# Inverse square roots by logarithm and exponential of one ScalarE table set, in a two-layer spectral MetaFormer

## The chip, the cores and the metric

One core of one Trainium2 chip runs the whole network in one launch. The metric is the device time of the program in microseconds; the median of three runs of the kernel before is 5417.38 us (5405.69 to 5420.78). The engines are named as in the profile: PE is TensorE's matmuls and PEld its weight loads, DVE is VectorE, ACT is ScalarE, POOL is GpSimd, SP is SyncE, which issues the DMAs.

## The reference

The input is eight images of 128 x 128 pixels with 96 channels. Two layers of the same form follow each other; for each:

```python
x = x + conv(_ln_c(x))                  # layer norm over the 96 channels, eps 1e-6
t = t + ffn(_ln_t(t))                   # layer norm over the 96 channels, eps 1e-5

# conv
x_pre = scale * relu(x @ w1.T)**2 + bias                   # 96 -> 192 channels
xf = rfft2(x_pre)
gctx = mean(x); sctx = mean(relu(bn(x @ sp_w.T)))           # over the pixels; bn uses rsqrt(bn_var + 1e-5)
r = softmax(fc2(soa(fc1([gctx, sctx]))), over 3 scales)     # one gate per image
comb = sum over the scales of r * filter
y = irfft2(xf * comb) @ w2.T

# ffn, every product in a quantised 8-bit float, sums in a quantised 16-bit one
y = fc2(relu(fc1(q(x)) + b1)) + b2
```

A layer norm is `(v - mean) / sqrt(var + eps)`. It needs one inverse square root per pixel, and there are 2 layers x 8 images x 16,384 pixels x 2 norms of them. The batch norm of the gate's context needs one inverse square root per channel and layer.

## The kernel before

The work is cut into 16 jobs (2 layers x 8 images), and each job into 16 groups of 8 image rows (`NRG = 16`). Four stages are written as generators whose `yield`s cut them into numbered steps:

- `pixels` (P): loads 8 rows, takes their statistics (L369), normalises on GpSimd (`xn_a`, L441), transposes (L445, read out on ScalarE, L448), multiplies by w1 (L456), takes ReLU (`r`, L459) and the square (`xs`, L463) on ScalarE, adds and subtracts rows (`sd`, L476/L477), and does the Fourier transform along one axis (L486, read out by ScalarE's `lo`, L500, and VectorE's `at`, L502/L503).
- `gate` (G): only at the last group of an image. Matmuls (L521 to L540), a softmax with an exponential on ScalarE (L551), sums on GpSimd (L554/L555), a reciprocal (L557) and the weights `rw` (L560 to L565) on VectorE.
- `frequencies` (F): the second axis of the transform (L627), the filters (L594, L614, read out by `cf`, L634), their complex products on VectorE (`pr`, L645 to L649) and GpSimd (`xf`, L657), the second projection (L698/L703, read out by `zt`, L713) and the inverse transform (L717). The last of the 16 chunks of an image has five columns in place of four.
- `tokens` (S): the last inverse transform (L746), the residual (L755) and its statistics, normalisation into 8-bit floats half on VectorE (L770) and half on ScalarE (L764), transposes (L778/L781), the feed-forward network (L788 to L814; `y` L791 and `h` L798 on ScalarE, `a` L794 on VectorE), and the output (L819).

A fifth list, `Norms.steps` (N), does the inverse square roots of a tick for P and S together, on tiles of 128 x 16 (or 128 x 8, when only one of the two is active). It has three steps. N 0 makes the variance on VectorE (L391 to L395). N 1 takes its square root on ScalarE (L397). N 2 takes the reciprocal on VectorE (L399), improves it with one Newton step (L401, L402, L407) and makes the shift for S (L405, L406).

The order of the work is written out by hand. One tick advances every stage by one group, and the lists `TICK`, `RAMP` and `TAIL` say which step of which stage is recorded in which place; `tc.manual_schedule()` keeps that order, so each engine runs its instructions in the order of the list. Stages lag behind each other by whole ticks (the third number of an entry), and `BANKS` gives each matmul output one of four PSUM bank pairs. In `TICK`, N 1 stands between the transposes' read-out (P 4) and ReLU (P 6):

```python
("P", 4, 1), ("G", 3, -1), ("N", 1, 0), ("P", 0, 3), ("P", 6, 0),
("P", 16, -1), ("N", 2, 0), ("S", 9, 0), ("G", 4, -1), ("P", 17, -1), ("P", 18, -1),
```

ScalarE evaluates Sqrt and Exp from tables, and the two lie in different table sets. So ACT_TABLE_LOAD instructions stand in the program wherever the function changes: one before the softmax's exponential of a gate (L551) and one before the next square root (L397), 16 of each, and one for the first square root of all, which is the batch norm's in the set-up (`prepare`, L268, with its reciprocal on L269).

Of the kernel before, what the change touches and what calls it, by code (L numbers as in the profile page):

```python
# [13 lines left out]
AF = mybir.ActivationFunctionType  # L14
# [160 lines left out]
def metaformer_kernel(ctx: ExitStack, tc: tile.TileContext, x, cst, layers, out):  # L175
    nc = tc.nc
# [8 lines left out]
    def bank2(name):  # L185
        return pp.tile([128, 2, 512], F32, name=name, tag=f"d{banks[name]}")

    ident = const.tile([128, 128], F32, name="ident")
    make_identity(nc, ident)
    ident8 = const.tile([128, 128], F8, name="ident8")  # L190
# [52 lines left out]
    def prepare(us, l, p):  # L243

        wt = {}

        def load(name, shape, view, pool=us):
            t = pool.tile(shape, F32, name=f"{name}_{l}" if pool is const else name)
            nc.sync.dma_start(t, view)
            return t  # L250

        def kept(name, shape, dtype=F32):
            wt[name] = const.tile(shape, dtype, name=f"{name}_{l}")
            return wt[name]

        def row(v, n):
            return v.partition_broadcast(n)


        K1 = C + 1  # L260
        gam = load("gam", [K1, SC], row(p["conv_bn_gamma"], K1))
        bet = load("bet", [K1, SC], row(p["conv_bn_beta"], K1))
        bmu = load("bmu", [K1, SC], row(p["conv_bn_mean"], K1))
        bva = load("bva", [K1, SC], row(p["conv_bn_var"], K1))
        bns = us.tile([K1, SC], F32, name="bns")
        t0 = us.tile([K1, SC], F32, name="bn_t0")
        nc.vector.tensor_scalar(bva, bva, 1e-5, None, ALU.add)
        nc.scalar.activation(t0, bva, AF.Sqrt)  # L268
        nc.vector.reciprocal(bns, t0)  # L269
        nc.vector.tensor_tensor(t0, bns, bns, ALU.mult)  # L270
        nc.vector.tensor_tensor(t0, t0, bva, ALU.mult)
        nc.vector.tensor_scalar(t0, t0, -0.5, 1.5, ALU.mult, ALU.add)
        nc.vector.tensor_tensor(bns, bns, t0, ALU.mult)
        nc.vector.tensor_tensor(bns, bns, gam, ALU.mult)
        nc.vector.tensor_tensor(t0, bmu, bns, ALU.mult)

        raw = us.tile([C, WE], F32, name="raw")
        nc.sync.dma_start(raw[:, :M], p["conv_w1"])
        spw = load("spw", [C, SC], p["conv_sp_w"])
        nc.vector.tensor_tensor(raw[:, M:], spw, bns[:C], ALU.mult)  # L280
        fc1g = load("fc1g", [C, RHID], p["conv_fc1"][:C, :])
        fc1s = load("fc1s", [SC, RHID], p["conv_fc1"][C:, :])

        cen = us.tile([C, C], F32, name="cen")
        nc.vector.tensor_scalar(cen, ident[:C, :C], -1.0 / C, None, ALU.add)
        ps = bank2("ps_w")
        mm(ps[:C, 0, :WE], cen, raw, start=True, stop=True)
        mm(ps[:C, 1, :RHID], cen, fc1g, start=True, stop=True)
        w1 = kept("w1", [K1, WE])
        nc.scalar.copy(w1[:C], ps[:C, 0, :WE])  # L290
        nc.vector.memset(w1[C:], 0.0)
        nc.vector.tensor_tensor(w1[C:, M:], bet[C:], t0[C:], ALU.subtract)
        nc.scalar.mul(kept("fc1g", [C, RHID]), ps[:C, 1, :RHID], 1.0 / (H * W))
        nc.scalar.mul(kept("fc1s", [SC, RHID]), fc1s, 1.0 / (H * W))
        nc.sync.dma_start(kept("fc2", [RHID, NS * M]), p["conv_fc2"])
        nc.sync.dma_start(kept("mlp_s", [RHID, 1]), row(p["conv_mlp_scale"], RHID))
        nc.sync.dma_start(kept("mlp_b", [RHID, 1]), row(p["conv_mlp_bias"], RHID))

        soa_s = load("soa_s", [128, 1], row(p["conv_soa1_scale"], 128))
        nc.vector.tensor_scalar(kept("dft", [128, 128]), kt["dft"], soa_s, None, ALU.mult)  # L300
        dc = kept("dc", [HH, 1])
        nc.sync.dma_start(dc, row(p["conv_soa1_bias"], HH))
        nc.vector.tensor_scalar(dc, dc, 2.0, None, ALU.mult)


        nc.sync.dma_start(kept("w2a", [128, C]), p["conv_w2"][:128, :])
        nc.sync.dma_start(kept("w2c", [128, C]), p["conv_w2"][64:, :])
        w2b = kept("w2b", [128, 2 * C])
        nc.vector.memset(w2b, 0.0)
        nc.sync.dma_start(w2b[:64, :C], p["conv_w2"][128:, :])  # L310
        nc.sync.dma_start(w2b[64:, C:], p["conv_w2"][:64, :])

        def quantised(name, shape, view):
            t = us.tile(shape, F32, name=f"{name}_f")
            nc.sync.dma_start(t, view)
            q = kept(f"{name}_q", shape, F8)
            nc.vector.tensor_copy(q, t, saturate=False)
            return q

        quantised("f1", [C, HID], p["ffn_W1"])  # L320
        quantised("f2", [128, HID // 128, C], p["ffn_W2"].rearrange("(k p) c -> p k c", p=128))
        b1q = quantised("b1", [128, HID // 128], p["ffn_b1"].rearrange("(k p) -> p k", p=128))
        b2q = quantised("b2", [128, C], p["ffn_b2"].partition_broadcast(128))
        nc.vector.tensor_copy(kept("b1", [128, HID // 128]), b1q)
        nc.vector.tensor_copy(kept("b2", [128, C], F16), b2q)
        return wt

    with tc.tile_pool(name="us", bufs=2) as us:
        pad = us.tile([NKW, GP - 2 * NHS, M], F32, name="pad", bufs=1)
        nc.gpsimd.memset(pad, 0.0)  # L330
        wts, cws = [], []
        for l, p in enumerate(layers):
            wts.append(prepare(us, l, p))
            cws.append(load_filters(us, l, p))
        constants("fwd", "inv", "idft", "rh", "mask")
        for l in range(len(layers)):
            small_filters(us, l, cws[l], pad)
# [21 lines left out]
    class Norms:  # L359
# [13 lines left out]
        def steps(self):  # L373

            if not self.slots:
                yield from [None] * 3
                return
            sl = slice(min(self.slots), max(self.slots) + 1)

            def new(name):  # L380
                return ab.tile([128, 2, RG], F32, name=f"n_{name}")

            add, mult = ALU.add, ALU.mult
            tt, stt = nc.vector.tensor_tensor, nc.vector.scalar_tensor_tensor
            me, mo = self.st[:, sl, :, 1], self.st[:, sl, :, 4]
            d, v, a, rs, nb = (new(i) for i in ("d", "v", "a", "rs", "nb"))
            sm = ab.tile([128, 2, RG, 2], F32, name="n_sm")
            self.sm, self.a, self.rs, self.nb = sm, a, rs, nb
            d, v, a, rs, sm = (i[:, sl] for i in (d, v, a, rs, sm))

            tt(sm, self.st[:, sl, :, 1:3], self.st[:, sl, :, 4:6], add)  # L391
            tt(d, me, mo, ALU.subtract)
            stt(v, d, 0.25, d, mult, mult)
            stt(v, sm[:, :, :, 1], 1.0 / C, v, mult, add)
            tt(v, v, eps[:, sl], add)  # L395
            yield
            nc.scalar.activation(a, v, AF.Sqrt)  # L397
            yield
            nc.vector.reciprocal(rs, a)  # L399

            stt(a, rs, -0.5, rs, mult, mult)  # L401
            tt(a, a, v, mult)  # L402
            if 1 in self.slots:
                nb = self.nb[:, 1]
                stt(nb, self.sm[:, 1, :, 0], -0.5, self.rs[:, 1], mult, mult)  # L405
                stt(nb, self.a[:, 1], 1.5, nb, add, mult)  # L406
            stt(rs, a, 1.5, rs, add, mult)  # L407
            yield
# [489 lines left out]
```

## Time and profile before

| what | before |
|---|---|
| median of three runs | 5417.38 us |
| span of the profiled execution | 5425.3 us |
| ACT_TABLE_LOAD | 33 of 1283 ns |
| Sqrt on L397 | 297, mean 219 ns |
| reciprocal on L399 | 297, mean 237 ns |
| exponential of the softmax, L551 | 16 of 684 ns |

The profile is of one execution. Its page gives the busy time of each engine, the span in 40 slices, the chain of waits that ended last, and the costliest groups of instructions. A group's row ends with the idle time of its engine just ahead of it and the instruction that ended it. An instruction in order of time that had to wait has that wait in square brackets, with what ended it. In a table of stretches each row has the stretch, its length, the busy time of TensorE, its weight loads, VectorE, ScalarE and GpSimd (with the instructions in brackets), the granted TensorE clock as a share of the full one, the share of the DMA engines, and GB/s. Line numbers are those of the kernel before.

### The profile page before, as it was taken

Reading aid. Unit: us, or ns where it says so; the run is one execution under the profiler, and the core shown is the slowest. Engines: PE = TensorE matmul, PEld = TensorE weight load, DVE = VectorE, ACT = ScalarE, POOL = GpSimd, SP = SyncE. Lnnn points to the kernel's source line nnn. Section 1 sums busy time; section 2 is a strip of 40 time slices with the busy share of each in tenths; the row PEclk is TensorE's granted clock in tenths of the full one; section 3 lists DMA queues with packets and bytes.
Section 4 is the critical chain, followed back from the end, with each engine's and each line's share of the span. In section 5 each row is a group of like instructions: output and inputs, shape, how many; then the busy total and the mean of one; then the engine's idle time right before and its main releaser. Section 6 shows DMA issues by size and latency. Waiting matters only on the chain.

```text
span 5425.3 us, 116490 instructions
## 1 busy us (share of the span) xinstructions
PE 5111.2 (94%) x41192; PEld 4031.7 (74%) x41192; DVE 4532.2 (84%) x14113; ACT 4400.2 (81%) x6882; POOL 2663.7 (49%) x1911
## 2 busy tenths in 40 slices
PE   4899999999999999999999999999999999998976
PEld 2577777878787787878778787877878787787743
DVE  3887888888888888888888888888888888888876
ACT  2654688888888888878888888888888888887778
POOL 0354555555555555545555555555555555554421
PEclk9999999999999999999999999999999999999987
DMA  5566777777676676767777776777777677766643
GB/s 143 163 163 156 182 197 193 205 190 210 184 209 196 192 206 182 212 179 202 205 199 201 189 212 183 208 197 196 201 191 212 177 209 199 197 195 174 179 122 108
DMA packets 908042, 1020.15 MB, mean 188 GB/s; under 512 B 67106, under 2 KB 839954, under 8 KB 907122
## 3 DMA queue, kind: packets, MB, share of 16 engines
q1 hardware_dynamic: 907460, 1012.71, 67.6%
q8 instruction: 327, 5.36, 0.4%
q14 instruction: 255, 2.09, 0.1%
HBM read 598.62 MB, written 413.84 MB: 187 GB/s over the span
## 4 chain that ended last, share of the span: by engine, by line
PE 73%; DVE 9%; issue 6%; ACT 5%; POOL 3%; DMA 2%; SPq 1%; POOLq 0%; DVEq 0%; ACTq 0%
PE pw L456 13%; PE py L627 12%; PE pf L614 7%; PE pz L703 6%; PE pi L717 6%; PE pz L698 6%; PE pa L486 5%; PE ps_r L746 5%; PE pm L788 5%; PE po L805 4%; PE pt_a L445 3%; PE pt_c L778 2%; DVE pr L645 1%; POOL ut L594 1%; DMA u_d<-u 1%
## 5 line engine op out<-in xcount | busy, mean ns | idle before, releaser
L657 POOL TENSOR_TENSOR xf<-pr 128x768 f32<-128x768 f32 (+2 forms) x544 | 957.9, 1764 | 320.6 <-DVE pr L649 280.7
L456 PE MATMUL pw<-w,xT 97*128 97x240 f32 x4096 | 935.2, 372 | 22.2 <-ACT y L791 14.0
L819 POOL TENSOR_TENSOR y<-xr,o 128x768 f32<-128x768 f32 x256 | 460.0, 1797 | 967.3 <-DVE o L816 930.4
L441 POOL TENSOR_TENSOR xn_a<-xt,n_rs 128x768 f32<-128x768 f32 x256 | 414.0, 1617 | 1016.8 <-DVE n_rs L407 832.5
L645 DVE TENSOR_TENSOR pr<-py,cf 128x768 f32<-128x768 f32 (+2 forms) x544 | 502.1, 923 | 469.3 <-PE py L627 430.3
L456 PEld LDWEIGHTS pw<-w,xT 97*128 97x128 f32 x4096 | 773.5, 194 | 154.3 <-ACT y L791 18.4
L627 PE MATMUL py<-k_fwd,al 128*128 128x128 f32 x6272 | 838.9, 283 | 1.7 <-ACT zt L713 1.7
L791 ACT CAST y<-pm 128x1024 f16<-128x1024 f32 x768 | 771.6, 1006 | 61.7 <-PE pm L788 60.9
L798 ACT ACTIVATE h<-a 128x1024 fp8e5<-128x1024 f16 x768 | 808.7, 1056 | 4.4 <-DVE a L794 3.7
L627 PEld LDWEIGHTS py<-k_fwd,al 128*128 128x128 f32 x6272 | 751.2, 193 | 43.7 <-issue 7.3
L459 ACT ACTIVATE r<-pw 128x960 f32<-128x960 f32 x512 | 496.4, 970 | 350.0 <-PE pw L456 349.9
L594 POOL TENSOR_TENSOR ut<-ut,rw 112x768 f32<-112x768 f32 (+1 forms) x256 | 490.0, 1914 | 317.3 <-DMA ut<-u_d 171.7
L698 PE MATMUL pz<-w2b,xf 128*128 128x192 f32 (+1 forms) x2112 | 553.8, 344 | 9.2 <-DVE hr L532 5.4
L788 PE MATMUL pm<-xq,f_q 96*128 96x512 fp8e5 x1536 | 474.3, 390 | 84.5 <-DVE pr L649 41.5
L698 PEld LDWEIGHTS pz<-w2b,xf 128*128 128x128 f32 (+1 forms) x2112 | 337.7, 190 | 185.1 <-issue 144.7
L614 PEld LDWEIGHTS pf<-k_rh,ut 48*128 48x128 f32 x6272 | 377.6, 190 | 119.1 <-issue 69.0
L794 DVE TENSOR_SCALAR a<-y,b 128x1024 f16<-128x1024 f16 x768 | 427.2, 556 | 43.9 <-ACT y L791 43.9
L614 PE MATMUL pf<-k_rh,ut 48*128 48x128 f32 x6272 | 433.4, 284 | 31.3 <-POOL ut L594 31.3
L463 ACT ACTIVATE xs<-r 128x768 f32<-128x768 f32 x512 | 428.1, 836 | 0.6
L634 ACT COPY cf<-pf 128x768 f32<-128x768 f32 (+2 forms) x544 | 399.8, 795 | 34.5 <-PE pf L614 34.4
L717 PE MATMUL pi<-zt,k_inv 128*128 128x384 f32 (+1 forms) x1024 | 423.0, 538 | 0.0
L781 ACT ACTIVATE xq<-pt_c 96x1024 fp8e5<-96x1024 f32 x256 | 260.9, 1019 | 181.0 <-PE pt_c L778 181.0
(126 smaller groups left out, 10648.8 us busy)
## 6 DMA issues: line engine op xcount, KB each, us to landing
a_d<-at SPq DMA_DIRECT2D x256, 768.0 KB
al<-a_d SPq DMA_DIRECT2D x960, 192.0 KB
v<-y_d SPq DMA_DIRECT2D x256, 384.0 KB
y_d<-yt SPq DMA_DIRECT2D x480, 192.0 KB
ut<-u_d SPq DMA_DIRECT2D x240, 336.0 KB
xt<-in_x_dram SPq DMA_DIRECT2D x512, 96.0 KB
xr<-in_x_dram SPq DMA_DIRECT2D x128, 384.0 KB
mid<-y SPq DMA_DIRECT2D x128, 384.0 KB
```

What stands on the lines that cost most here:

```text
L456: mm(o, xT[:, 4 * a + 2 * i + j, :], wt["w1"], start=True, stop=True)
L459: nc.scalar.activation(r.rearrange("p a s c -> p a (s c)"), pw, AF.Relu)
L594: nc.gpsimd.tensor_tensor(ut[:, :n], ut[:, :n], _bc_mid(jb.rw, n), ALU.mult)
L614: mm(pf[:nm, i, t * 128 : (t + 1) * 128], utf[64 * i : 64 * i + NHS, cs], kt["rh"][64 * i : 64 * i + NHS, :], start=True, stop=True,)
L627: mm(py[:nm, t, e, :], alf[:, e, cs], kt["fwd"][:, e, :], start=True, stop=True)
L645: nc.vector.tensor_tensor(p0, yq, crb, ALU.mult)
L657: nc.gpsimd.tensor_tensor(xv[:q, te], pr[:q, 0, te].rearrange("p t r k -> p t (r k)"), pr[:q, 1, te].rearrange("p t r k -> p t (r k)"), AL ...
L698: mm(o[:, : u * C], xf[:kb, 1, e, :], wt["w2b"][:kb, : u * C], start=True, stop=False,)
L717: mm(pi[:, e, : n * C], kt["inv"][:, e, :], zt[:, e, : n * C], start=True, stop=True)
L788: mm(pm[:, s, :], fk, xq[:, s, :], start=True, stop=True)
L791: nc.scalar.copy(y16, pm)
L798: nc.scalar.activation(hk, a16, AF.Copy, saturate=False)
```

## The change

Ln and Exp lie together in one of ScalarE's table sets, and `1/sqrt(v)` is `exp(-0.5 * ln(v))`. The change names that set once at the start and takes every inverse square root by Ln and Exp on ScalarE, in the layer norms and in the batch norm of the set-up. Square root and reciprocal go; the Newton step on VectorE stays. The softmax's exponential is then served by the same set, so that no table has to be loaded between norms and gates. In `Norms.steps` both activations stand in N 1, where the square root stood.

```diff
+    nc.scalar.preload_act_table_set("natural_log_exp_and_others")
     ident = const.tile([128, 128], F32, name="ident")
...
         nc.vector.tensor_scalar(bva, bva, 1e-5, None, ALU.add)
-        nc.scalar.activation(t0, bva, AF.Sqrt)
-        nc.vector.reciprocal(bns, t0)
+        nc.scalar.activation(t0, bva, AF.Ln)
+        nc.scalar.activation(bns, t0, AF.Exp, scale=-0.5)
...
             yield
-            nc.scalar.activation(a, v, AF.Sqrt)
-            yield
-            nc.vector.reciprocal(rs, a)
+            nc.scalar.activation(rs, v, AF.Ln)
+            nc.scalar.activation(rs, rs, AF.Exp, scale=-0.5)
+            yield
```

In the built program one table load is left, at the start. The order on TensorE and SyncE is the same, and so is that of all other instructions on ScalarE and VectorE. Ln now writes the tile `n_rs`, which GpSimd's normalisation (L441) reads, so ScalarE takes over a wait for that reader.

## The prediction

> **What bounds the kernel now.** I read the page's first two parts, then a table of stretches, the groups of instructions by line, the chain of waits, and the engines in order of time.
>
> ```profile
> PE 5111.2 (94%) x41192; PEld 4031.7 (74%) x41192; DVE 4532.2 (84%) x14113; ACT 4400.2 (81%) x6882; POOL 2663.7 (49%) x1911
> PEclk9999999999999999999999999999999999999987
> ```
>
> TensorE is the busiest engine, at a clock that is nearly always whole. The busy time of stretches says where its missing 6% lies. The first row is nine ordinary ticks, the second is everything between ramp and tail:
>
> ```profile
> 2202.00:2370.00 168.00, 168.00 (x1423) 135.96 (x1421) 147.19 (x471) 150.11 (x234) 90.33 (x65) 1.00 0.75 208
> 600.00:4950.00 4350.00, 4251.85 (x35123) 3399.39 (x35120) 3748.17 (x11687) 3726.77 (x5801) 2279.40 (x1629) 0.99 0.72 198
> ```
>
> In ordinary ticks TensorE is busy for 168.00 of 168.00 us: nothing done to another engine shortens them. Taking the start of the addition on L395 as a mark, ordinary ticks follow each other at 18.7 us. Over the long stretch TensorE is idle for 98 us, some 7 us for each of the 14 images in it, and the marks show where: two ticks per image, those of the gate, last 23.4 to 28.5 and 27.6 to 29.0 us. Both sets of table loads fall in the first of the two. The groups of the instructions concerned, from the groups by line of ScalarE and of VectorE:
>
> ```profile
> L397 ACT ACTIVATE n_a<-n_v 128x16 f32<-128x16 f32 (+1 forms) x297 | 65.0, 219 | 55.7 <-DVE n_v L395 55.4
> L551 ACT ACT_TABLE_LOAD x16 | 20.5, 1283 | 0.3
> L397 ACT ACT_TABLE_LOAD x16 | 20.5, 1283 | 0.3
> ```
>
> ```profile
> L399 DVE RECIPROCAL n_rs<-n_a 128x16 f32<-128x16 f32 (+1 forms) x297 | 70.5, 237 | 76.3 <-ACT n_a L397 64.4
> ```
>
> The 64.4 us that the reciprocal waits for are 51 waits of at most 2.8 us; 16 of them, at the gates, are most of the sum. The chain of waits through one gate tick (start, us, what) has both loads on it:
>
> ```profile
> 2077.04 1.02 ACT xq L781
> ...
> 2078.81 1.28 ACT L551
> ...
> 2084.95 1.28 ACT L397
> ...
> 2086.24 0.23 ACT n_a L397
> 2086.47 0.02 issue
> 2086.49 0.26 DVE n_rs L399
> ```
>
> It goes on through VectorE's queue (L401 to L407, L794, L502/L503, L557, then the products L645 to L649) to TensorE, whose records in order of time show the two gaps of this tick:
>
> ```profile
> 2082.68 1.89 PE L456 MATMUL pw<-w,xT 97*128 97x240 f32 x8 [1.08 <-ACT y L791]
> ...
> 2094.28 1.03 PE L788 MATMUL pm<-xq,f_q 96*128 96x512 fp8e5 x2 [2.83 <-DVE pr L649]
> ```
>
> The first load makes y late (1.08 us of idle TensorE), both together make the products late (2.83 us). The gate tick at 1445 to 1457 us has the same two gaps, 1.08 and 2.83.
>
> [...] L463 ends at 2078.79, the load begins at 2078.81 and the exponential at 2080.10. So I price a switch at 1.28 to 1.3 us[...]. [...] Nothing before uses that set; in the built program only the one load stays. [...] the stretch 2092.5 to 2099.4, which begins inside the 2.83 us gap, has a granted clock of 0.51.
>
> **The change part by part.**
>
> *Table loads.* 32 of 33 go, 32 x 1.283 = 41.1 us of ScalarE; the 33rd moves to the very start, where the chain is DMA. How much of 2.57 us per image reaches TensorE? ScalarE's queue moves up 1.28 us from L551 on, so y is ready in time, and the 1.08 us gap closes: TensorE ends its py matmuls at 2090.37 in place of 2091.45. The logarithm can start at about 2083.6 (n_v is ready at 2083.39, xT read out by 2083.5), the exponential ends at about 2084.0, and L401 starts at 2084.05 in place of 2086.78: 2.7 us earlier. VectorE is free from 2083.78 (the 2.71 us wait before L399 begins there), so it takes this. Its queue then runs 2.7 us earlier until the products of the last unit, which need the py matmuls: 2090.4 in place of 2092.70, 2.2 to 2.3 us earlier. TensorE's pm follows, at about 2092.1 in place of 2094.28. I take 2.2 us, x 16 = -35 us. Bounds: 1.1 (only the first gap) and 2.6 (all) per image, -17 to -41.
>
> *The added Exp.* Before does not show this shape. The nearest row is the Sqrt of the same size, 219 ns; the 112x576 exponential takes 684 ns, the same 0.83 ns per element and start-up[...]. It waits for Ln to finish (in VectorE's dependent chain L393 to L395 such a wait costs 0.03 us), so +0.25 us; bounds 0.13 (queued without a wait, as L397 to L459 at 2111.78 to 2111.91) and 0.4. 297 x 0.25 = 74 us of ScalarE. Behind it in ScalarE's queue stand r (L459) and lo (L500), and TensorE waits for these through banks. In an ordinary tick:
>
> ```profile
> 2019.46 0.22 ACT L397 ACTIVATE n_a<-n_v 128x16 f32<-128x16 f32 x1
> 2019.97 0.97 ACT L459 ACTIVATE r<-pw 128x960 f32<-128x960 f32 x1 [0.28 <-PE pw L456]
> ```
>
> r waits 0.28 us for TensorE anyway, so Exp lies in that wait: 0 us. For VectorE L401 comes at the same time as before, since the 0.25 us reciprocal goes. In the second gate tick ScalarE stands 1.00 us for n_v and a later TensorE wait of 0.33 us hangs on its queue; there Exp costs its 0.25: 16 x 0.25 = +4 us.
>
> *The removed reciprocals.* 70.5 us of VectorE, worth nothing where TensorE is full. In the first ramp (13 ticks of 6.6 us) VectorE works back to back, so 13 x 0.23 = -3 us. The batch-norm pair in the set-up and the preload lie behind the DMA of the filters, which carries the chain to 112 us: 0.
>
> *Tail.* From 5240 to 5425 us ScalarE is busy for 163.18 of 185 us. It often waits 0.7 us for po right after L397, which takes Exp in; in other ticks it does not. 20 ticks x 0.15 = +3 us, bounds 0 and 9 (36 ticks x 0.25).
>
> *Writing Ln to n_rs.* Two ScalarE instructions now also wait for the reader of the buffer two ticks back (GpSimd, L441), done about a tick before: 0.
>
> *Clock.* The 2.83 us gap shrinks to some 1.7. After it the clock is halved for 3.4 to 6.9 us, costing 1.7 to 2.5 us. With a shorter gap I expect this to be saved at about 5 of 14 gates: 5 x 2 = -10 us; bounds 0 and -30.
>
> Sum: -35 + 4 - 3 + 3 - 10 = -41; 5417 - 41 = 5376 us.
>
> **The rivals.**
> - *The clock gives more.* If no gate tick is halved after the change, -30 in place of -10: 5356 us. For it: TensorE's gaps add up to 3.9 us before and 1.7 after. Against: gates also halve the clock after two earlier gaps of about 1.1 and 0.7 us (2068.6 to 2072.1 at 0.51), which stay.
> - *A wait takes the load's place.* If VectorE's queue does not move as far as ScalarE's, because lo, cf or GpSimd's sums hold it, only the first gap closes: 16 x 1.08 = -17, +4 for Exp: 5404 us. For it: the ut multiplication waits 7.5 us per image for rw, so the gate is a web of waits. Against: rw itself is at the end of the same VectorE queue, and no wait stands between L401 and L557.
> - *Exp hits the ordinary ticks, and the kernel is slower.* If each of the 193 ordinary ticks takes 0.25 us more: +48, tail +9, gates +4, loads -35, ramp -3 = +23: 5440 us. For it: TensorE has no slack there at all, and ScalarE is 89% busy (150.11 of 168). Against: ScalarE waits for TensorE at r, zt and xq in every tick (349.9, 126.0 and 181.0 us in sum), so it catches up.
>
> **How the numbers follow.** Forecast 0.60, more from the clock 0.17, a wait in its place 0.17, Exp in ordinary ticks 0.06. The bounds (loads 1.1 to 2.6 per image, clock 0 to -30, tail 0 to 9) spread the forecast over about 5350 to 5400; the range to 5406 takes in the second rival, and 5347 most of the first. Faster by over 0.3% means below 5401: 0.60 + 0.17 + 0.03 of the second rival = 0.80; slower 0.06; within 0.14.
>
> **What would show it.** Right: one table load; L401 waits for ScalarE by 0.3 us at most at the gates; the gap before pw gone and that before pm near 1.7 us; ordinary ticks still 18.7 us and full; gate pairs shorter by 2 us or more. Wrong: ordinary ticks above 18.75 us, a new TensorE wait for r or lo, or gate ticks that halve the clock more often [...]. The last is the weakest point[...].

## The result, and the profile after

The changed kernel takes 5369.4 us (5364.5 to 5377.3) against 5419.0 us of before (both medians of four runs; ahead of the prediction there were three of before): a ratio of 0.9915, 95% interval 0.9895 to 0.9935. Forecast were 5376 us, with a range of 5347 to 5406. The profiled execution has a span of 5367.8 us, 57.5 less than the one of before. The change adds two lines ahead of L397, so a line of the norms is two or more further down (Ln is L399, Exp L400, the first multiplication of the Newton step L403).

The first two parts of the page:

```profile
PE 5075.2 (95%) x41192; PEld 4013.8 (75%) x41192; DVE 4474.8 (83%) x13814; ACT 4420.0 (82%) x7149; POOL 2651.8 (49%) x1911
...
PEclk7999999999999999999999999999999999999987
```

ScalarE is busy for 20 us more, VectorE for 57 us less, and TensorE, with the same 41192 matmuls, for 36 us less. TensorE also worked for less long at the halved clock, 47.0 us in place of 95.7 in the ticks between ramp and tail; that is the first sign of what the forecast had too small. How much of it is lasting is told further down.

Groups by line of ScalarE, and of VectorE:

```profile
L399 ACT ACTIVATE n_rs<-n_v 128x16 f32<-128x16 f32 (+1 forms) x297 | 65.0, 219 | 55.8 <-DVE n_v L397 39.2 <-DMA xt<-in_x_dram 16.2
L400 ACT ACTIVATE n_rs<-n_rs 128x16 f32<-128x16 f32 (+1 forms) x297 | 63.4, 214 | 9.4
...
L189 ACT ACT_TABLE_LOAD x1 | 1.3, 1283 | 0.7 <-PEq L867 0.7
```

```profile
L403 DVE SCALAR_TENSOR_TENSOR n_a<-n_rs 128x16 f32<-128x16 f32 (+1 forms) x297 | 51.2, 172 | 93.5 <-ACT n_rs L400 88.8
```

One table load is left. Ln costs what Sqrt cost (219 ns), Exp 214 ns. VectorE still waits for ScalarE, now for Exp: 88.8 us in 221 waits, at most 1.9 us, where it was 64.4 us in 51 waits of up to 2.8 us. These are mostly short waits (0.4 us on average) in ordinary ticks, where VectorE has time.

A table of stretches, nine ordinary ticks of after:

```profile
2180.00:2348.00 168.00, 168.00 (x1419) 135.35 (x1416) 144.65 (x461) 151.97 (x243) 90.60 (x65) 1.00 0.74 207
```

TensorE is as full as before, and the median ordinary tick is 18.712 us in both. ScalarE in order of time in one such tick:

```profile
2000.57 0.22 ACT L399 ACTIVATE n_rs<-n_v 128x16 f32<-128x16 f32 x1
2000.82 0.21 ACT L400 ACTIVATE n_rs<-n_rs 128x16 f32<-128x16 f32 x1
2001.08 0.97 ACT L461 ACTIVATE r<-pw 128x960 f32<-128x960 f32 x1
```

ReLU starts 0.51 us after Ln starts, and it started 0.51 us after Sqrt (2019.46 to 2019.97). Exp stands where ScalarE waited for the matmuls.

Now a gate tick. ScalarE's records around the places of the two loads, and TensorE's wait that is left:

```profile
2056.09 0.83 ACT L465 ACTIVATE xs<-r 128x768 f32<-128x768 f32 x1
2056.83 0.67 ACT L553 ACTIVATE lg<-lg 112x576 f32<-112x576 f32 x1
...
2061.43 0.21 ACT L450 ACTIVATION_READ_ACCUMULATOR xT<-pt_a 96x1 f32 x1
2061.52 0.22 ACT L399 ACTIVATE n_rs<-n_v 128x16 f32<-128x16 f32 x1
2061.78 0.21 ACT L400 ACTIVATE n_rs<-n_rs 128x16 f32<-128x16 f32 x1
```

```profile
2069.95 0.60 PE L790 MATMUL pm<-xq,f_q 96*128 96x512 fp8e5 x2 [1.70 <-DVE pr L651]
```

The 1.08 us wait ahead of the pw matmuls (L458 now) is gone, and 2.83 us ahead of pm have become 1.70.

**Where the 57.5 us went.** The start to the first norm gave 1.0, the ramp up to the 45th norm 3.3, the tail from the 257th norm on 4.9, and the 212 ticks between 48.3. For those ticks the table of stretches has, before and then after:

```profile
675.35:4869.83 4194.48, 4104.14 (x33939) 3281.72 (x33939) 3616.57 (x11290) 3609.93 (x5617) 2206.26 (x1575) 0.99 0.72 198
```

```profile
671.05:4817.28 4146.23, 4078.13 (x33939) 3268.81 (x33939) 3563.81 (x11077) 3622.52 (x5803) 2195.72 (x1575) 0.99 0.72 200
```

Length less TensorE's busy time is its idle time: 90.3 us before, 68.1 after. The trace's record of the granted clock shows it at one half while TensorE is busy for 95.7 us before and 47.0 after; half of that I count as lost, an estimate from the one half. Length less idle less half of that is 4056.3 and 4054.6 us, the work at the whole clock by this estimate, the same in both. So of 48.3 us, 22.2 are idle time, 24.4 are clock, and 1.6 are left over. The clock's part has two sources. Sorted by the gap that it follows, the halved clock behind pm is 58.1 us before and 33.3 after; behind an earlier gap of 1.2 us ahead of po, which the change leaves as it was, it is 37.5 and 13.7. Half of each difference: 12.4 and 11.9 us. I use this sum, over the same ticks, for every experiment.

### The profile page after: what moved, and what is told of

It reads as the page before. It is cut to its first block, busy times and chain, and to the rows that moved or that the text cites. A ratio compares the mean times of both kernels' runs of the same rounds, so it can differ in the third digit from the quotient of the medians.

```text
span 5367.8 us, 116350 instructions
## 1 busy us (share of the span) xinstructions
PE 5075.2 (95%) x41192; PEld 4013.8 (75%) x41192; DVE 4474.8 (83%) x13814; ACT 4420.0 (82%) x7149; POOL 2651.8 (49%) x1911
## 4 chain that ended last, share of the span: by engine, by line
PE 76%; DVE 8%; issue 6%; POOL 4%; ACT 3%; DMA 1%; SPq 1%; POOLq 0%; DVEq 0%; ACTq 0%
PE pw L458 13%; PE py L629 13%; PE pf L616 7%; PE pz L705 7%; PE pz L700 6%; PE pa L488 6%; PE pi L719 6%; PE ps_r L748 5%; PE pm L790 5%; PE pt_a L447 4%; PE po L807 3%; PE pt_c L780 2%; POOL ut L596 1%; DVE pr L647 1%; POOL y L821 1%
## 5 line engine op out<-in xcount | busy, mean ns | idle before, releaser
L458 PE MATMUL pw<-w,xT 97*128 97x240 f32 x4096 | 925.1, 369 | 13.2 <-ACT xT L450 12.0
L458 PEld LDWEIGHTS pw<-w,xT 97*128 97x128 f32 x4096 | 765.4, 192 | 136.4 <-ACT xT L450 22.8
L793 ACT CAST y<-pm 128x1024 f16<-128x1024 f32 x768 | 770.8, 1005 | 58.3 <-PE pm L790 57.5
L719 PE MATMUL pi<-zt,k_inv 128*128 128x384 f32 (+1 forms) x1024 | 407.6, 522 | 0.0
```

The source lines that it names most:

```text
L458: mm(o, xT[:, 4 * a + 2 * i + j, :], wt["w1"], start=True, stop=True)
L719: mm(pi[:, e, : n * C], kt["inv"][:, e, :], zt[:, e, : n * C], start=True, stop=True)
L793: nc.scalar.copy(y16, pm)
```

## The experiments

All were timed beside the kernel before on the same chip. In the list, idle and halved are TensorE's idle time and its busy time at the halved clock in the 212 ticks (13 gates), work is the sum's remainder; the gaps are the median ones at a gate, ahead of pw and of the pm that waits for the products.

| kernel | us (median) | ratio to before, 95% | 212 ticks | idle | halved | work | gap pw | gap pm |
|---|---|---|---|---|---|---|---|---|
| before | 5419.0 | 1 | 4194.5 | 90.3 | 95.7 | 4056.3 | 1.08 | 2.83 |
| after | 5369.4 | 0.9915 (0.9895-0.9935) | 4146.2 | 68.1 | 47.0 | 4054.6 | none | 1.70 |
| loads only | 5375.0 | 0.9926 (0.9899-0.9954) | 4151.5 | 69.6 | 53.7 | 4055.0 | none | 1.70 |
| both loads back | 5422.0 | 1.0012 (1.0001-1.0023) | 4209.3 | 96.4 | 109.2 | 4058.3 | 1.08 | 2.84 |
| first load back | 5384.4 | 0.9946 (0.9926-0.9967) | 4167.3 | 85.0 | 47.3 | 4058.6 | 1.08 | 1.70 |
| second load back | 5398.2 | 0.9968 (0.9958-0.9978) | 4181.9 | 78.5 | 100.1 | 4053.4 | none | 2.84 |
| copy added to before | 5440.5 | 1.0049 (1.0031-1.0067) | 4210.6 | 98.7 | 106.2 | 4058.8 | 1.08 | 2.87 |
| ramp's N 1 earlier | 5368.9 | 0.9916 (0.9888-0.9945) | 4162.2 | 71.4 | 72.5 | 4054.6 | none | 1.71 |
| banks exchanged | 5372.4 | 0.9919 (0.9888-0.9951) | 4155.3 | 76.0 | 47.6 | 4055.5 | none | none |
| banks exchanged in before | 5405.6 | 0.9983 (0.9973-0.9994) | 4179.4 | 103.8 | 29.7 | 4060.7 | 1.08 | none |
| banks, rw sooner | 5369.6 | 0.9919 (0.9892-0.9945) | 4144.0 | 71.8 | 23.9 | 4060.3 | none | none |
| banks, reciprocal on ScalarE | 5325.3 | 0.9837 (0.9814-0.9860) | 4119.1 | 48.7 | 30.7 | 4055.0 | none | none |
| the same, old banks | 5376.9 | 0.9928 (0.9902-0.9955) | 4168.9 | 70.3 | 91.1 | 4053.0 | none | 1.86 |
| banks, reciprocal, ramp | 5323.5 | 0.9828 (0.9796-0.9861) | 4120.7 | 48.7 | 34.1 | 4054.9 | none | none |

Where no gap stands ahead of pm, there are others, told below. Work is 4053 to 4061 us in all of them, and a median ordinary tick 18.711 or 18.712 us. The columns from the fifth on are of one profiled execution each, which need not lie at the median of its kernel: that of the banks exchanged in before took 5383.6 us, the least of its 20 runs.

**Loads only.** The loads go from the kernel before, and nothing else: the square root becomes a copy, which brings no load of its own (with a copy added to the kernel before, further down, there are 33 loads, as without it). It leaves out the square root, in norms and set-up.

```diff
+    nc.scalar.preload_act_table_set("natural_log_exp_and_others")
...
-            nc.scalar.activation(a, v, AF.Sqrt)
+            nc.scalar.activation(a, v, AF.Copy)
```

> Before, with the square root replaced by a plain copy, so that no set but one is ever needed and 32 loads go; the reciprocal stays and no exponential is added. It leaves out the square root, so its numbers are not the norms'. My theory (all of the gain is the loads at the gates): ordinary ticks 18.71 us, ramp ticks 6.63 us as before, TensorE gaps at a gate 1.70 us as after, time 5360 to 5370 us. Rival (part of the gain is the 70 us that VectorE no longer spends on reciprocals): 5380 us or more.

5375.0 us, 5 us above what I expected and 5 us below the rival's bound, which its interval (to 0.9954, 5392 us) takes in; it overlaps that of the changed kernel. So the times alone don't settle it, and the profile has to: idle time is 69.6 us against 68.1. The ramp tick is 6.640 us and the gap ahead of pm 1.70. With the reciprocals still there and no exponential added, the gate ticks are those of after:

```profile
2062.33 0.60 PE L789 MATMUL pm<-xq,f_q 96*128 96x512 fp8e5 x2 [1.70 <-DVE pr L650]
```

Within what times and profile tell, the loads are all of the gain; the exchange of reciprocal for exponential is worth nothing either way.

**Both loads, and one at a time, put back.** The changed kernel, with the set loaded again at a gate: ahead of the softmax's exponential (first), ahead of the tick's Ln (second), or both.

```diff
+        nc.scalar.preload_act_table_set("natural_log_exp_and_others")
         nc.scalar.activation(lg, lg, AF.Exp)
+        reload[0] = True
...
+            if reload[0]:
+                nc.scalar.preload_act_table_set("natural_log_exp_and_others")
+                reload[0] = False
             nc.scalar.activation(rs, v, AF.Ln)
```

> The changed kernel with both loads of every gate put back (the same set loaded again). My theory: the gaps of 1.08 and 2.83 us at each gate and the halved clock return, ramp ticks stay at 6.8 us: 5415 to 5426 us. Rival (the relief of VectorE counts): below 5405 us.

> The changed kernel with only the load ahead of the softmax's exponential put back. My theory: the pw matmuls wait 1.08 us for y again, py and the products end 1.1 us later, so pm is 1.1 us later; with half of the clock's share 5390 to 5400 us. Rival 1 (both loads lie on one chain that only the sum makes late): below 5378 us. Rival 2 (this load alone makes the gate late): above 5408 us.

> The changed kernel with only the load ahead of the gate tick's logarithm put back. My theory: the gap ahead of pw stays closed, VectorE's queue starts 1.28 us later, of which 0.15 us are slack, so the gap ahead of pm grows from 1.70 to 2.8 us: 5388 to 5402 us. Rival 1: below 5378 us. Rival 2 (this load alone makes the gate late): above 5408 us.

Both: 5422.0 us, as before (1.0001 to 1.0023), with VectorE still relieved of its reciprocals. So the relief, with Exp in its place, counts for nothing. TensorE in one of its gate ticks:

```profile
2079.72 1.89 PE L463 MATMUL pw<-w,xT 97*128 97x240 f32 x8 [1.08 <-ACT y L800]
...
2091.45 0.77 PE L797 MATMUL pm<-xq,f_q 96*128 96x512 fp8e5 x2 [2.84 <-DVE pr L658]
```

First alone, 5384.4 us, and second alone, 5398.2 us; TensorE in a gate tick of each:

```profile
2066.43 1.89 PE L458 MATMUL pw<-w,xT 97*128 97x240 f32 x8 [1.08 <-ACT y L794]
...
2076.90 1.04 PE L791 MATMUL pm<-xq,f_q 96*128 96x512 fp8e5 x2 [1.70 <-DVE pr L652]
```

```profile
2077.76 1.04 PE L796 MATMUL pm<-xq,f_q 96*128 96x512 fp8e5 x2 [2.84 <-DVE pr L657]
```

The two loads cost TensorE different things, as expected: the first one gap, because py and the products then move together, the second the growth of the other. In idle time the first costs 16.9 us and the second 10.4. But the first one alone was 6 us cheaper than I expected, because the clock took no part: halved for 47.3 us, as after. The second brought the halved clock back whole, 100.1 us: half of the 53 more is 26.6 us. Not all of that is the load's: behind pm the halved clock is 59.2 us in place of 33.3, and behind po, whose gap the load leaves at 1.2 us, 41.0 in place of 13.7. So 13.0 us of clock come with the 2.84 us gap, which only the second load makes, and the rest is how the gaps of this one execution fell. With 10.4 of idle time they are 23.4 us in 13 gates, or 29 in 16, which is the difference of the medians (5398.2 less 5369.4).

**The added instruction alone.** A copy behind the square root in the kernel before, with reciprocals and loads kept.

```diff
             nc.scalar.activation(a, v, AF.Sqrt)
+            nc.scalar.activation(a, a, AF.Copy)
```

> Before, with a plain copy on ScalarE added right behind the square root, where the exponential stands in the changed kernel; loads and reciprocals stay. It prices the added ScalarE instruction alone. My theory: ordinary ticks stay at 18.71 us, ramp ticks go from 6.63 to 6.8 us or a little more, time 5417 to 5427 us. Rival (ordinary ticks pay for it): ticks of 18.96 us, 5465 us or more.

Ordinary ticks are free of it (18.712 us), and ramp ticks go to 6.811 us, both as expected. The time does not: 5440.5 us, 0.3 to 0.7% above before, where I expected 0.2% at most, and its runs spread from 5421 to 5463. The link of 0.25 us is now added to a chain that keeps its reciprocal, and it shows at the gates: in the one seen in order of time, the wait ahead of po is 1.48 us. A gate of before, and then of this kernel:

```profile
1745.43 1.18 PE L805 MATMUL po<-f_q,h 128*128 128x96 fp8e5 x24 [1.21 <-DVE at L503]
```

```profile
2057.58 1.18 PE L806 MATMUL po<-f_q,h 128*128 128x96 fp8e5 x24 [1.48 <-DVE at L504]
```

In the 212 ticks 8.4 us are idle time and 5.3 (half of 10.5) clock. The sum over the ticks does not account for the whole difference of the medians. In the changed kernel, Exp (216 ns for 128x16) does not cost this, since it takes the place of a reciprocal of about equal length (252 ns) on the same chain: there the median wait ahead of po is 1.18 us.

**The ramp.** The ramp's N 1 is recorded ahead of the second ReLU.

```diff
-    ("P", 5, 1), ("P", 17, -1), ("P", 18, -1), ("P", 2, 2), ("P", 11, 0), ("N", 1, -1),
+    ("P", 5, 1), ("P", 17, -1), ("P", 18, -1), ("P", 2, 2), ("N", 1, -1), ("P", 11, 0),
```

> The changed kernel with the logarithm and exponential of the ramp recorded one place earlier, ahead of the second ReLU (N 1 before P 11), where ScalarE waits 1.3 us for matmuls. My theory (in the ramp the exponential delays the square, and VectorE waits 0.22 us for it): ramp ticks go from 6.81 to 6.6 us or less, that wait goes, everything else stays; time 5 us less at most, 5360 to 5372 us. Rival (the ramp is slower for another reason, such as the loads of x): ticks stay at 6.81 us.

Ramp ticks go from 6.814 to 6.617 us, a little under those of before (6.633), and the time, 5368.9 us, cannot tell. In the ramp VectorE waited for the square (`xs`) in 12 ticks, 8.2 us in all, of which 5.1 are a first one; the other eleven are 0.2 to 0.3 us each. VectorE's waits from 130 to 225 us, of after and then of this kernel:

```profile
DVE sd L478 <- ACT xs L465: 8.2, 12, 5.1
```

```profile
DVE sd L478 <- ACT xs L465: 5.7, 2, 4.9
```

So Exp stood ahead of the square in ScalarE's queue, and VectorE, which had been back to back, waited for it in every tick. This kernel has the gate gaps of after, and yet its halved clock is 72.5 us and not 47.0: some 13 us of clock differ between two profiles of the same gates, 10 of them behind po (34.1 us halved against 13.7).

**The bank ahead of pm.** pm1 lies in the PSUM bank pair 0, which py2, the fifth column's transform, leaves only when VectorE has multiplied it. Exchanged with pf2:

```diff
-    "pm1": 0, "pm2": 1, "po": 3, "pf2": 2, "py2": 0, "pz2": 2,
+    "pm1": 0, "pm2": 1, "po": 3, "pf2": 0, "py2": 2, "pz2": 2,
```

> The changed kernel with the PSUM banks of the fifth column's pf and py exchanged (pf2 in 0, py2 in 2), so that pm no longer waits for the last products of a gate tick. My theory: the gap of 1.70 us ahead of pm is gone and with it the halved clock that follows it (24 us of idle TensorE and some 10 us of clock in ticks 44 to 256, a little more at the ends): 5325 to 5342 us. Rival (the next wait, of po or pi, takes its place): 5355 us or more.

> Before, with the same exchange of banks; the 32 loads stay. It asks how much of a load's price is that one bank. My theory: the gap ahead of pm goes or shrinks below 1 us, the 1.08 us gap ahead of pw stays, and the halved clock behind pm goes: 5417 less 30 idle and 25 clock, 5355 to 5380 us. Rival (other waits on the late VectorE queue take over, po above all): 5400 us or more.

The rivals' times held, both times, though the waits that they named (po, pi) are the smaller part: pf, which neither named, waits longest. After the change the time stays (5372.4 us); TensorE in a gate tick:

```profile
2078.69 1.53 PE L719 MATMUL pi<-zt,k_inv 128*128 128x384 f32 x4 [0.23 <-DVE pr L651]
...
2084.15 1.61 PE L616 MATMUL pf<-k_rh,ut 48*128 48x128 f32 x24 [2.31 <-POOL ut L596]
```

The gap is only taken a few matmuls later: pf needs ut, ut needs rw, and rw stands behind reciprocal, products and `xn_c` in VectorE's queue. In the kernel before, the same edit gave 5405.6 us: its pw gap stays, and pi and pf wait in place of pm (12.4 and 34.4 us in the 212 ticks). TensorE is idle for 13.5 us more than before, and at the halved clock for 66 us less; but the profile is of the fastest of 20 runs, so the 66 us are likely more than a median run has.

**rw sooner, and the reciprocal on ScalarE.** With the banks exchanged, either only G 11 goes ahead of the feed-forward normalisation, or the gate's reciprocal is taken by Ln and Exp too, ahead of F 7, with rw right behind it:

```diff
-        nc.vector.reciprocal(den, den)
+        nc.scalar.activation(den, den, AF.Ln)
+        nc.scalar.activation(den, den, AF.Exp, scale=-1.0)
...
-    ... ("F", 13, 0), ("F", 14, 0), ("F", 7, 1), ("S", 10, 0),
-    ("P", 7, 0), ("P", 19, -1), ("G", 10, -2), ("F", 8, 1), ("F", 9, 1), ("P", 2, 2), ("S", 3, 1),
-    ("G", 11, -2), ("F", 1, 2), ...
+    ... ("F", 13, 0), ("F", 14, 0), ("G", 10, -2), ("F", 7, 1), ("S", 10, 0),
+    ("P", 7, 0), ("P", 19, -1), ("G", 11, -2), ("F", 8, 1), ("F", 9, 1), ("P", 2, 2), ("S", 3, 1),
+    ("F", 1, 2), ...
```

> The changed kernel with the banks of pf2 and py2 exchanged, and with the gate's last step (rw) recorded right behind the last products instead of behind the feed-forward normalisation (G 11 ahead of P 2 and S 3). My theory (with the banks exchanged, pf waits 2.31 us for ut, and ut waits for rw): rw is ready 1.0 us sooner, the gap ahead of pf goes from 2.31 to about 1.3 us, 13 us less of idle TensorE and some of the halved clock: 5345 to 5362 us. Rival (xn_c, now later, makes its own matmuls late): 5368 us or more.

> The changed kernel with the banks of pf2 and py2 exchanged, the gate's reciprocal (1.34 us of VectorE) taken as logarithm and exponential on ScalarE from the set that is loaded anyway, recorded ahead of F 7, and rw recorded right behind it, ahead of the last products. My theory: rw is ready 5 us sooner, the gap of 2.31 us ahead of pf goes, the products end 0.8 us later and pi waits about 1 us for them: 1.5 us less idle TensorE per gate than with the exchange alone, and less of the halved clock: 5335 to 5355 us. Rival (VectorE now waits for ScalarE ahead of the products, and the gap only moves to pi and po): 5365 us or more.

> The changed kernel with the gate's reciprocal on ScalarE and rw ahead of the last products, but with the old banks (pf2 in 2, py2 in 0). My theory (pm waits for the products through the bank, and they now end 0.8 us later): the gap ahead of pm grows from 1.70 to about 2.5 us and the halved clock follows it more often: 5372 to 5395 us. Rival (the exchange of banks was no part of the gain): 5320 to 5335 us.

> The changed kernel with the exchanged banks, the gate's reciprocal on ScalarE with rw ahead of the last products, and the ramp's logarithm and exponential one place earlier. My theory: the gate ticks are as without the last edit, ramp ticks 6.62 in place of 6.81 us, 2 to 3 us less: 5315 to 5330 us. Rival (the parts disturb each other[...]): 5335 us or more.

rw sooner alone only moved the gap once more, to the time that its rival gave, though not to the matmuls of xn_c that it named. rw is ready 1.0 us sooner, as expected; the ut multiplication behind it also took 1.86 us in place of 2.98, which I had not expected and leave open. The wait ahead of pf is 0.23 us, but ps_r and pm, which hang on VectorE's later work, wait in its place:

```profile
2075.10 1.61 PE L616 MATMUL pf<-k_rh,ut 48*128 48x128 f32 x24 [0.23 <-POOL ut L596]
...
2079.96 1.56 PE L748 MATMUL ps_r<-v,k_idft 128*128 128x384 f32 x4 [1.28 <-DVE yt L726]
...
2084.35 0.59 PE L790 MATMUL pm<-xq,f_q 96*128 96x512 fp8e5 x2 [0.88 <-DVE xr L757]
```

With 1.34 us of reciprocal off VectorE and rw ahead of the products the web of waits opens: 5325.3 us, 10 us under the lowest that I expected. A gate tick of TensorE, and the two new ScalarE groups:

```profile
2055.36 1.53 PE L720 MATMUL pi<-zt,k_inv 128*128 128x384 f32 x4 [0.39 <-DVE pr L652]
...
2071.86 0.43 PE L701 MATMUL pz<-w2b,xf 64*128 64x96 f32 x2 [0.44 <-DVE at L505]
```

```profile
L559 ACT ACTIVATE mx<-mx 112x192 f32<-112x192 f32 x16 | 5.9, 369 | 0.0
L560 ACT ACTIVATE mx<-mx 112x192 f32<-112x192 f32 x16 | 5.8, 363 | 0.5
```

Two activations of 0.37 us, in a tick in which ScalarE has time, for one reciprocal of 1.34 us in a tick in which VectorE holds TensorE. In one gate of each, seen in order of time, rw is ready 5.6 us sooner after the softmax's exponential than with the exchange alone (9.97 against 15.55), and the products end only 0.15 us later (13.22 against 13.06), not the 0.8 that I expected: rw went ahead of them, and the reciprocal left. No run has rw ahead of the products with the reciprocal still on VectorE, so how much the new order alone is worth is not shown. With the old banks the pair is worth nothing (5376.9 us): pm waits 1.86 us for the products, where I expected 2.5. So neither the exchange of banks nor this pair is worth anything without the other. With the ramp's edit as well it is 5323.5 us, no different in the times; the ramp tick is 6.620 us. This is the best kernel of the study, 1.7% under before (0.9796 to 0.9861).

## Why the prediction was right, point by point

- **What bounds it.** Right. Ordinary ticks are TensorE's alone: 18.711 or 18.712 us in all fourteen kernels, whatever was added to ScalarE or taken from VectorE. The whole effect lies in gate ticks and ends.
- **A switch is 1.28 us.** Right for this queue: every load in the profiles of before, after and both loads back takes 1283 ns, and with each load put back alone, its gap is 1.08 or 1.14 (2.84 less 1.70) us wider, neither over 1.28.
- **Loads, -35 us (2.2 per gate).** Right. The gap ahead of pw went from 1.08 to none and that ahead of pm from 2.83 to 1.70, as worked out: 2.21 per gate, 28.7 in 13 gates. The idle time as a whole fell by 22.2, since pf and smaller waits took 6.5 back. pf's share is 0.94 or 0.95 us in each of the four gates whose gap ahead of pm the halved clock did not follow, so a clock that is spared there is about half eaten by the next wait. In the four kernels with the gap of 1.70 us it is the same at all 19 such gates.
- **Exp at gates, +4 us.** Wrong, though small: the wait that I gave it to (pz in the second gate tick) adds up to 3.8 us in the 13 gates before and to 3.2 after. I counted the added 0.25 us and not the 0.25 us of reciprocal that leave the same chain. With the copy added and the reciprocal kept, that wait adds up to 6.7 us.
- **Reciprocals in the ramp, -3 us.** Wrong in sign: the step failed where it took VectorE as the only limit of the ramp. A loop through ScalarE was as tight, Exp lengthened it, and ramp ticks went up by 0.18 us, 2.5 us in 14 ticks. Moving Exp by one place undid it.
- **Tail, +3 us.** About nothing: the last 16 ticks take 153.36 us in place of 153.45. One profile of each cannot exclude 3 us: before with the banks exchanged, whose norms are the same, has 150.31.
- **Clock, -10 us.** That fewer of the shorter gaps would be followed by the halved clock was right, though the 5 of 14 was an estimate that the profile of before did not show, and the size was nearly so; the rest of the 24.4 us in the profiles is luck. Before, the halved clock follows all 14 gaps ahead of pm, seven times for 3.4 us and seven times for 6.8. After, it follows 10 of 14, nine times for 3.4 us and once for 6.8: four gates are spared where I expected five, and the others are halved for less long, 12.4 us in the 13 gates. I also held the halved clock behind the gate's earlier gaps, ahead of po, for unchanged; it followed 7 of 7 such gaps before and 2 of 8 after, which is the other 11.9 us. The change left these gaps at 1.2 us, so I put this down to where they fell among the steps of 3.41 us (see the last section), and it is not lasting: with the same gaps, the kernel with the ramp's edit has it after 6 of 11. 24 us is thus one draw; with that kernel's clock it would have been about 12.

Exp and tail were taken too dear by 7 us, the ramp too cheap by 5.5, the waits that took 6.5 us back were not in the sum, and the clock was too small by 14, of which 12 are the draw at po. By these sizes the forecast is 9 us short. So it is of the difference of the medians (49.6 us), but the sizes were read in two executions that differ by 57.5, so that agreement is in part luck too; the 212 ticks leave 9.2 us of the 57.5 to start, ramp and tail, which I did not take apart further. Of the rivals, a wait in the load's place would have cost half the gain and did not come; the slower one, Exp in ordinary ticks, is refuted by the tick itself.

What stays open: why the copy added to before costs 0.5% in the timed runs and 5 us in the profiled span. The mean granted clock of its ten runs is 0.9715, and 0.9739 in the 29 of before beside them, which points to the clock but does not show it.

## What to carry to other kernels

Price a table load by the gap that it opens on the bound engine, not by its own length, and add what the clock does after that gap: here each load of 1.28 us widened one gap by 1.1 us, and the load that made a gap of 2.8 us cost more again in clock (13.0 us in 13 gates) than in idle time (10.4). Clock that one profile shows behind gaps that did not change is not part of the price. An instruction that is added to an engine with time is free only if it lengthens no chain; look for what leaves the same chain, and look at ramp and tail as stages of their own. Where one tick is a web of waits, removing one of them moves the gap to the next, until the work that they all hang on gets shorter.

## What the runs showed of the hardware that was not expected

- Longer gaps were followed by the halved clock more often, and gaps of one length not always. Those of 2.65 to 2.90 us ahead of pm were followed by it in all 41 cases (before, both loads back, second load back), those of 1.85 us and more of the old banks with the reciprocal on ScalarE in 13 of 14, those of 1.70 us in 33 of 52 (after, loads only, first load back, ramp's N 1 earlier). But the gaps of 2.31 us ahead of pf, with the banks exchanged, were followed in 9 of 13 gates of the changed kernel and in only 4 of 13 of the kernel before.
- From 600 to 4900 us before has 20 halved stretches and after 12, each 3.41 or 6.83 us long. In each of the two profiles they all start and end whole multiples of 3.41 us apart, within 0.01 us, and so divide it into steps of that length. TensorE's idle time (by its matmul records) can be summed over each such step at the whole clock. Of 2391 steps with less than 0.8 us idle none was followed by a halved step, of 63 with 0.8 to 1.8 us 16 were, and of 16 with 1.8 us and more all 16. The same sums over all 14 profiles give none of 16,796, 107 of 469 and 89 of 89. Of the 26 gaps of 2.31 us, the 12 with 1.62 us or more in one step were all followed, of the other 14 one. These are counts of these executions; what lies behind them was not shown.
- Ln and Exp of 128x16 take 223 and 216 ns, Sqrt of the same size 223; Exp behind a Ln that it needs starts 0.25 us after it (2000.57 and 2000.82).
- VectorE's reciprocal of 112x192 takes 1340 ns; the same by Ln and Exp on ScalarE takes 369 and 363 ns.
